# A transformer block with windowed attention and routed experts: the first block's program order, and scatters tied to steps

## The chip, the cores and the metric

The kernel runs on one core of a Trainium2 chip. Its engines work beside each other, each through its own queue in order: TensorE (PE) for matrix products, VectorE (DVE) and ScalarE (ACT) for elementwise work and reductions, GpSimd (POOL), and SyncE (SP), which here only issues transfers. The metric is device time in microseconds (us); the time before is 508.23, the median of six runs from 506.51 to 510.97.

## The reference

The input is x, 2048 rows of 256 values. A vector c gives six modulation vectors of 256. Cut to what matters:

```
mod = (silu(c) @ wmod).reshape(1, 6, 1, -1)
sa, ca, ga, sb, cb, gb = ...            # ga, gb are kept away from zero
h = layernorm(x) * (1 + ca) + sa
x = x + ga * attention(h)               # 16 heads of 16, windows of 64 rows
h = layernorm(x) * (1 + cb) + sb
x = x + gb * (experts(h) + shared(h))   # 16 experts, each row goes to 4
```

In the attention each chunk of 64 rows looks at itself and the chunk before. The experts are gated two-layer networks with 176 hidden values; the router chooses four of 16 for each row, with a weight. The shared network has 352 hidden values and takes every row.

## The kernel before

The rows are worked in four blocks of 512 (`NB`), each as four tiles of 128 rows (`NT`). The kernel is written as one stream of instructions; a framework then decides in which order each engine gets them, by dependences, by a model of when inputs are ready and by the place in the program. So an instruction that is ready early can stand on its engine ahead of others that come before it in the program. Waits between engines are added by the framework.

**Constants and loads** (L114 to L290): masks, identity matrices, counters, then the loads on SP's queue, then `sc`, the silu of c.

**`norm_t`** (L227) is a generator. It takes statistics of a block's four tiles (`bn_stats`, `bn_aggr`, L233 and L234, DVE), yields, takes the square root on ACT (L236) and the reciprocal on DVE, writes `xn` (L241), yields, and per half of 128 columns transposes on PE (L249) and writes `hT` on ACT with the modulation's shift and scale (L250). `half` is 0 for the norm ahead of the attention and 1 for the one ahead of the experts.

**`shift_scale`** (L299) computes shift and scale of one half: 16 matmuls (L304), two DVE instructions that write `mod` (L310, L311).

**`front(b)`** (L352) runs `norm_t` and then the projections of block b: queries (L363, evicted by DVE L368 and ACT L369), keys (L374, L378) and values (L393, evicted by ACT L397 and DVE L398, L399). They share two PSUM buffers of the tag "mm".

**The attention loop** (L683) has 16 units per block, 64 in all. `scores(u)` handles two units: a mask matmul each (L450) and the products (L456). `softmax(u)` takes row maxima into `top` (L472, four buffers), subtracts them or hands them to ACT, and takes the exponential (L477, L485). `total`, `turn_p`, `spread`, `turn_s`, `values` and `heads_out` finish the heads. Beside the units the loop advances two generators by one step or two: `nexts`, which is `front` of the next block, and `ends`, which is first `gates` (the second half of the modulation and the gate vectors) and then `back` of the block before.

**`back(b)`** (L556) applies the output projection, norms again, routes the rows and computes for each row and choice a place `at` (L658) in the table `slots` in memory. A row of `slots` holds 256 normed values, 16 weights and four words for the token number: `RW` is 276, and only the first of the four is read later. Sixteen indirect transfers per block (four tiles, four choices, L664) scatter the rows `row` into `slots` from POOL's queue, with a yield ahead of every second one. The helper `apart` tells the framework that these do not depend on each other.

**After the loop** (L712 to L765) the expert weights `wgu` are loaded, and `shared(b)` (L403), the shared network of blocks 0 to 2, is advanced as the generator `side`, two steps for each step of `ends`; its matmuls are L413 and L424. Then the rows per expert are counted and a table of expert blocks is made.

**The expert stage** (L768 to L891): SP fills the ends of the expert lists with blank rows (L788), loads blocks of 128 rows from `slots` (`xr`, L803), each load behind all writes of `slots`. The shared network of block 3 runs, then 79 expert blocks: transpose (L814), up (L832), transpose (L846), down (L854), and an indirect transfer from POOL that adds the result into one of two sums (L861). At the end the sums are read back and added to x (L900 to L912).

Of the kernel before, what the change touches and what calls it, by code (L numbers as in the profile page):

```python
# [8 lines left out]
F32 = mybir.dt.float32  # L9
# [8 lines left out]
P = 128  # L18
# [5 lines left out]
NT = TB // P  # L24
# [6 lines left out]
def adaln_block_kernel(  # L31
# [17 lines left out]
    nc = tc.nc  # L49
    S = x.shape[0]  # L50
    NB = S // TB
    NE = extra_scale.shape[1]
    TOPK = 4
# [7 lines left out]
    RS = S + P  # L61
    NBLK = S * TOPK // P + NE - 1
    RW = E + NE + 4
# [9 lines left out]
    xs = []  # L73
# [37 lines left out]
        return w.rearrange("(k p) n -> p k n", p=P)  # L111


    ident = const.tile([P, P], F32, name="ident")  # L114
    make_identity(nc, ident)
    eps_b = const.tile([P, 1], F32, name="eps_b")
# [5 lines left out]
    for par in range(2):  # L122
# [9 lines left out]
        out=mask[0:W], in_=mask[0:W], compare_op=ALU.is_ge, fill=NEG, base=0,  # L132
# [3 lines left out]
        out=mask[0:W], in_=mask[0:W], compare_op=ALU.is_ge, fill=NEG, base=W,  # L136
# [10 lines left out]
    for h in range(2):  # L147
# [7 lines left out]
        out=before, in_=before, compare_op=ALU.is_gt, fill=0.0, base=0,  # L155
# [38 lines left out]
    slots = dram.tile([RS * NE + P, RW], F32, name="slots")  # L194
# [4 lines left out]
    def apart(ins, name):  # L199

        ins = getattr(ins, "ins", ins)
        tc.declare_no_dep(ins, group=name, reason="no two of these write one row")
        tc.add_to_no_dep_group(name, ins)
        written[name].append(ins)
# [22 lines left out]
    def norm_t(pool, psum, xb, half, dst, xn=None):  # L227

        mv = pool.tile([P, NT, 2], F32, tag="mv", name="mv")
        rstd = pool.tile([P, NT], F32, tag="rstd", name="rstd")  # L230
        for t in range(NT):
            st = pool.tile([P, 6], F32, tag="st", name="st")
            nc.vector.bn_stats(st, xb[:, t, :])  # L233
            nc.vector.bn_aggr(mv[:, t, :], st)  # L234
        yield
        nc.scalar.activation(rstd, mv[:, :, 1], AF.Sqrt, bias=eps_b[:, 0:1])  # L236
        nc.vector.reciprocal(rstd, rstd)
        if xn is None:
            xn = pool.tile([P, NT, E], F32, tag="xn", name="xn", bufs=1)
        for t in range(NT):  # L240
            nc.vector.tensor_scalar(  # L241
                xn[:, t, :], xb[:, t, :], mv[:, t, 0:1], rstd[:, t : t + 1],
                ALU.subtract, ALU.mult,
            )
        for k in range(KC):
            yield
            ps = psum.tile([P, NT, P], F32, tag="mm", name="ps_xt")
            for t in range(NT):
                nc.tensor.transpose(ps[:, t, :], xn[:, t, k * P : (k + 1) * P], ident)  # L249
            nc.scalar.activation(  # L250
                dst[:, k, :], ps[:, :, :].rearrange("p t q -> p (t q)"), AF.Identity,
                bias=mod[:, 3 * half, k : k + 1], scale=mod[:, 3 * half + 1, k : k + 1],
            )
# [29 lines left out]
    for acc in sums_of:  # L283
        nc.sync.dma_start(
            out=acc[:, :].rearrange("(n p) e -> p n e", p=P),
            in_=blank[:, 0:E].unsqueeze(1).to_broadcast([P, S // P + 1, E]),
# [12 lines left out]
    def shift_scale(psum, half):  # L299
        ps = psum.tile([P, 2, KC], F32, tag="mm", name="ps_mod")  # L300
        for i in range(2):
            for m in range(KC):
                for k in range(KC):
                    nc.tensor.matmul(  # L304
                        ps[:, i, m : m + 1],
                        lhsT=wmod_at(3 * half + i, k)[:, m * P : (m + 1) * P],
                        rhs=sc[:, k : k + 1],
                        start=(k == 0), stop=(k == KC - 1),
                    )
        nc.vector.tensor_copy(mod[:, 3 * half, :], ps[:, 0, :])  # L310
        nc.vector.tensor_scalar(mod[:, 3 * half + 1, :], ps[:, 1, :], 1.0, None, ALU.add)  # L311
# [29 lines left out]
    with ExitStack() as actx:  # L341
        wa = actx.enter_context(tc.tile_pool(name="wa", bufs=2))
# [60 lines left out]
        def shared(b, hidden, psum):  # L403

            hs = []
            for j in range(SJ):
                n = min(P, SH - j * P)
                h = hidden()
                hs.append(h)
                pg, pu = psum(), psum()  # L410
                for ps, w in ((pg, sg), (pu, su)):
                    for k in range(KC):
                        nc.tensor.matmul(  # L413
                            ps[0:n], lhsT=w[:, k, j * P : j * P + n], rhs=hT[b][:, k, :],
                            start=(k == 0), stop=(k == KC - 1),
                        )
                    yield
                nc.scalar.activation(h[0:n], pg[0:n], AF.Silu)
                nc.vector.tensor_tensor(h[0:n], h[0:n], pu[0:n], ALU.mult)
            for t in range(NT):  # L420
                ps = psum()[:, 0:E]
                for j in range(SJ):
                    n = min(P, SH - j * P)
                    nc.tensor.matmul(  # L424
                        ps, lhsT=hs[j][0:n, t * P : (t + 1) * P], rhs=sd[0:n, j, :],
                        start=(j == 0), stop=(j == SJ - 1),
                    )
                nc.vector.tensor_tensor(xs[b][:, t, :], ps, xs[b][:, t, :], ALU.add)
                yield

        UNITS = 4 * 2 * KC
        probs, sums, turned, scale, av, outs = {}, {}, {}, {}, {}, {}

        def where(u):

# [24 lines left out]
        def softmax(u):  # L464

            g, r = divmod(u, 4)
            s = probs[u]
            if r == 0:
                sums[g] = wa.tile([P, 4, 4], F32, tag="sum", name="sum")
            alone = r % 2 == 1  # L470
            top = wa.tile([P, 4], F32, tag="top", name="top", bufs=4)
            nc.vector.tensor_reduce(top, s, AX.X, ALU.max, negate=alone)  # L472
            sm = wa.tile([P, 4, 2 * W], F32, tag="sm", name="sm", bufs=4)
            probs[u] = sm
            if alone:
                for n in range(4):
                    nc.scalar.activation(  # L477
                        sm[:, n, :], s[:, n, :], AF.Exp, bias=top[:, n : n + 1],
                        accum_out=sums[g][:, n, r : r + 1],
                    )  # L480
                return
            nc.vector.tensor_tensor(
                sm, s, top[:, :].unsqueeze(2).to_broadcast([P, 4, 2 * W]), ALU.subtract
            )
            nc.scalar.activation(sm, sm, AF.Exp)  # L485
# [70 lines left out]
        def back(b):  # L556

            oT = outs.pop(b)
            for t2 in range(NT // 2):
                ps = ps_mm.tile([P, 2, E], F32, tag="mm", name="ps_a")  # L560
                for t in range(2):
                    at = (2 * t2 + t) * P
# [94 lines left out]
            at = wr_.tile([P, NT, TOPK], I32, tag="at", name="at", bufs=2)  # L657
            nc.vector.tensor_scalar(at, keys[:, :, 0:TOPK], -1.0, BIG, ALU.mult, ALU.add)  # L658
            nc.vector.tensor_tensor(row[:, :, E : E + NE], sr, chosen, ALU.mult)
            for t in range(NT):  # L660
                for i in range(TOPK):
                    if i % 2 == 0:
                        yield
                    ins = nc.gpsimd.indirect_dma_start(  # L664
                        out=slots[:, :],
                        out_offset=bass.IndirectOffsetOnAxis(ap=at[:, t, i : i + 1], axis=0),
                        in_=row[:, t, :],
                        in_offset=None,
                        bounds_check=RS * NE - 1,
                    )  # L670
                    apart(ins, "slots")


        heads = {}
        shift_scale(ps_mm, 0)
        for _ in front(0):
            pass
        last = NB * UNITS
        scores(0)
        softmax(0)  # L680
# [2 lines left out]
        for u in range(last + 3):  # L683
            if u % UNITS == 0 and u // UNITS + 1 < NB:
                nexts = front(u // UNITS + 1)
            if u % 2 == 0 and u + 2 < last:
                if (u + 2) % UNITS == 0:
                    for _ in nexts:
                        pass
                scores(u + 2)  # L690
            if u + 2 < last:
                softmax(u + 2)
            if u < last:
                total(u)
                turn_p(u)
            g, r = divmod(u, 4)
            if r == 3 and u < last:
                spread(g)
            if r == 0 and g > 0:
                turn_s(g - 1)  # L700
            if r == 1 and g > 0:
                values(g - 1)
            if r == 2 and g > 0:
                heads_out(g - 1)
                if g % (UNITS // 4) == 0:
                    for _ in ends:
                        pass
                    ends = back(g // (UNITS // 4) - 1)
            next(nexts, None)
            for _ in range(2 if r == 3 else 1):  # L710
                next(ends, None)
        nc.sync.dma_start(out=wgu, in_=w_gu_t.rearrange("(k p) e n -> p k e n", p=P))  # L712


# [8 lines left out]
        side = beside()  # L723
        for _ in ends:
            next(side, None)
            next(side, None)


        ps = ps_mm.tile([P, NE], F32, tag="mm", name="ps_n")
# [224 lines left out]
```

## Time and profile before

| | |
|---|---|
| median of six runs | 508.23 us |
| the profiled execution | 507.85 us |
| its span | 506.1 us |
| mean granted PE clock | 0.972 |
| first softmax instruction | 29.42 us |
| first reduction of units 16, 32, 48 | 70.5, 120.7, 169.9 us |
| scatters on POOL | 114.4 to 266.2 us, in four runs of sixteen |
| first `xr` load issued | 278.23 us |
| expert blocks on PE | about 281 to 479 us, 2.49 us each |

The span runs from the program's first instruction to its last; what the device's time has beyond it lies around it. All places in the text are microseconds from the start of the span. In the lines of the profile an engine's name is followed by the kernel's line, the instruction, what it writes and reads, the number of instructions merged (x), and in brackets the idle time of that engine just before and what ended it. PEld is PE's loading of weights, which runs beside its products. In the table of stretches the columns are the stretch, its length, and the busy time of each engine with the number of its instructions, then the granted PE clock, the share of the transfer engines and GB/s.

### The profile page before, as it was taken

How to read it: one execution, taken by the hardware profiler on the slowest of the kernel's cores; microseconds unless marked ns; L12 is line 12 of the kernel's file. 1: busy time of each engine (PE TensorE's matmuls, PEld its weight loads, DVE VectorE, ACT ScalarE, POOL GpSimd, SP SyncE). 2: the span in 40 equal slices, each digit the busy share in tenths (PEclk: the TensorE clock that was granted, in tenths of full speed). 3: DMA queues.
4: the chain of work that ended last, by engine and by line, in shares of the span. 5: the costliest groups of instructions: out<-in, count | busy, mean ns of one | idle time of the engine just before them, and what ended most of it. 6: DMA issues, size and time to landing. Idle time of an engine off the chain costs nothing.

```text
span 506.1 us, 9444 instructions
## 1 busy us (share of the span) xinstructions
PE 455.9 (90%) x2903; PEld 323.1 (64%) x2921; DVE 337.4 (67%) x913; ACT 226.2 (45%) x623; POOL 191.7 (38%) x166
## 2 busy tenths in 40 slices
PE   3999979998998899899999999999999999999900
PEld 3475766666766577556554677777777777777600
DVE  4599789789969898755333566666666666666515
ACT  2377687958866878742001233333333333333100
POOL 2002000007501730362470165756556566656720
PEclk9999999999999899999999999999999999999955
DMA  8968000002200310194135497677777767765487
GB/s 277 328 151 286 17 1 2 1 1 93 90 1 12 113 58 2 52 418 166 57 111 191 97 154 124 113 112 115 108 104 114 107 106 111 114 97 62 55 239 289
DMA packets 52563, 58.87 MB, mean 116 GB/s; under 512 B 16363, under 2 KB 48331, under 8 KB 52171
## 3 DMA queue, kind: packets, MB, share of 16 engines
q1 hardware_dynamic: 36435, 35.72, 25.5%
q0 software_dynamic: 14448, 19.41, 22.1%
q10 hardware_dynamic: 1632, 3.15, 1.7%
q8 instruction: 24, 0.39, 0.3%
q14 instruction: 24, 0.20, 0.1%
HBM read 29.90 MB, written 28.35 MB: 115 GB/s over the span
## 4 chain that ended last, share of the span: by engine, by line
PE 60%; DMA 18%; DVE 13%; ACT 5%; issue 3%; DVEq 0%; SPq 0%; POOLq 0%; ACTq 0%; POOL 0%
DMA sum<-y,xr 15%; PE pgu L832 12%; PE py L854 8%; PE pz L413 8%; PE pz L424 4%; PE pt L497 3%; PE s L456 3%; DVE top L472 3%; PE ps_q L363 3%; ACT sm L477 2%; PE px L814 2%; PE ph L846 2%; PE ps_a L564 2%; DMA got<-sum 2%; PE ps_k L374 2%
## 5 line engine op out<-in xcount | busy, mean ns | idle before, releaser
L861 POOL DMA_INDIRECT sum<-y,xr x79 | 122.2, 1547 | 96.4 <-DVE xT L820 41.5
L664 POOL DMA_INDIRECT slots<-row,at x64 | 63.0, 985 | 156.5 <-DVE at L658 109.0
L832 PE MATMUL pgu<-wgu,xT 128*128 x316 | 106.5, 460 | 0.4 <-DVE xT L820 0.4
L854 PE MATMUL py<-wd,hT 88*128 x316 | 81.4, 379 | 0.1
L816 ACT ACTIVATE xT<-px,mod 128x128 f32<-128x128 f32 x79 | 36.1, 457 | 81.4 <-PE px L814 79.3
L832 PEld LDWEIGHTS pgu<-wgu,xT 128*128 128x128 f32 x316 | 53.8, 190 | 17.4 <-ACT xT L816 0.7
L848 DVE COPY hT<-ph 88x256 f32<-88x256 f32 x79 | 33.2, 421 | 39.8 <-PE ph L846 39.8
L854 PEld LDWEIGHTS py<-wd,hT 88*128 88x128 f32 x316 | 53.6, 190 | 4.8 <-DVE hT L848 0.5
L838 ACT ACTIVATE h<-pgu 128x176 f32<-128x176 f32 x79 | 25.1, 317 | 59.3 <-PE pgu L832 59.3
L477 ACT ACTIVATE sm<-s,top 128x128 f32<-128x128 f32 x128 | 45.8, 371 | 10.8 <-DVE top L472 10.8
L497 PE MATMUL pt<-ident,sm 128*128 128x128 f32 x256 | 40.9, 282 | 7.4 <-ACT sm L485 6.1
L820 DVE TENSOR_SCALAR xT<-px,mod 128x128 f32<-128x128 f32 x79 | 32.4, 410 | 22.2 <-ACT xT L816 22.2
L499 ACT COPY pT<-pt 128x512 f32<-128x512 f32 x64 | 37.5, 593 | 19.0 <-PE pt L497 18.6
L472 DVE TENSOR_REDUCE top<-s 128x4 f32<-128x512 f32 x64 | 42.1, 681 | 2.9 <-PE s L456 2.6
L456 PEld LDWEIGHTS s<-wgu 32*128 32x128 f32 x512 | 31.8, 186 | 16.0 <-issue 15.6
L860 DVE TENSOR_TENSOR y<-py,gate 128x256 f32<-128x256 f32 x79 | 33.6, 425 | 11.7 <-PE py L854 1.0
L456 PE MATMUL s<-wgu 32*128 32x128 f32 x512 | 39.0, 285 | 0.1
L497 PEld LDWEIGHTS pt<-ident,sm 128*128 128x128 f32 x256 | 28.9, 141 | 15.7 <-ACT sm L485 7.3
L846 PEld LDWEIGHTS ph<-ident,h 128*88 128x88 f32 x158 | 19.4, 123 | 21.9 <-issue 13.5
L839 DVE SCALAR_TENSOR_TENSOR h<-h,by,pgu 128x176 f32<-128x176 f32 x79 | 30.3, 384 | 1.3 <-ACT h L838 1.3
L814 PE MATMUL px<-ident,xr 128*128 128x128 f32 x158 | 30.4, 273 | 0.3 <-DMA xr<-slots 0.3
L846 PE MATMUL ph<-ident,h 128*88 128x128 f32 x158 | 30.2, 273 | 0.0
(166 smaller groups left out, 670.2 us busy)
## 6 DMA issues: line engine op xcount, KB each, us to landing
xr<-slots SPq DMA_DIRECT2D x79, 138.0 KB
wgu<-in_w_gu_t SPq DMA_DIRECT2D x1, 5632.0 KB
sum<-blank SPq DMA_DIRECT2D x2, 2176.0 KB
wd<-in_w_down_t SPq DMA_DIRECT2D x1, 2816.0 KB
slots<-blank SPq DMA_DIRECT2D x17, 138.0 KB
x<-in_x SPq DMA_DIRECT2D x4, 512.0 KB
got<-sum SPq DMA_DIRECT2D x4, 512.0 KB
got<-sum ACTq DMA_DIRECT2D x4, 512.0 KB
```

What stands on the lines that cost most here:

```text
L413: nc.tensor.matmul(ps[0:n], lhsT=w[:, k, j * P : j * P + n], rhs=hT[b][:, k, :], start=(k == 0), stop=(k == KC - 1),)
L456: nc.tensor.matmul(probs[u + i][:, n, :], lhsT=qz[at, m, ch].rearrange("p h q -> p (h q)"), rhs=kT[at, m, ch * W : (ch + 2) * W], start=False,
L472: nc.vector.tensor_reduce(top, s, AX.X, ALU.max, negate=alone)
L477: nc.scalar.activation(sm[:, n, :], s[:, n, :], AF.Exp, bias=top[:, n : n + 1], accum_out=sums[g][:, n, r : r + 1],)
L497: nc.tensor.transpose(pt[:, n, :], p[:, n, :], ident)
L499: nc.scalar.copy(turned[u], pt)
L664: ins = nc.gpsimd.indirect_dma_start(out=slots[:, :], out_offset=bass.IndirectOffsetOnAxis(ap=at[:, t, i : i + 1], axis=0), in_=row[:, t, ...
L814: nc.tensor.transpose(ps[:, k, :], xr[b][:, k * P : (k + 1) * P], ident)
L832: nc.tensor.matmul(ps, lhsT=xT[b][:, k, :], rhs=wgu[:, k, bass.ds(e, 1), :].rearrange("p e n -> p (e n)"), start=(k == 0), stop=(k == KC - 1),
L846: nc.tensor.transpose(ps[:, c2, :], h[b][:, c2 * DH : (c2 + 1) * DH], ident)
L854: nc.tensor.matmul(ps, lhsT=hT2[b][:, c2, :], rhs=wd[:, c2, bass.ds(e, 1), :].rearrange("p e n -> p (e n)"), start=(c2 == 0), stop=(c2 == 1),)
L861: nc.gpsimd.indirect_dma_start(out=sums_of[b % NA][:, :], out_offset=bass.IndirectOffsetOnAxis(ap=xr[b][:, E + NE : E + NE + 1].bitcast(I3 ...
```

## The change

Cut to its core:

```diff
+    first_order = ctx.enter_context(ExitStack())
+    first_order.enter_context(tc.manual_schedule(
+        engines={mybir.EngineType.PE, mybir.EngineType.DVE, mybir.EngineType.Activation}
+    ))
     ident = const.tile([P, P], F32, name="ident")
...
-            nc.vector.bn_stats(st, xb[:, t, :])
+            ins = nc.vector.bn_stats(st, xb[:, t, :])
+            if half == 0 and xb is not xs[0]:
+                tc.keep_in_program_order(ins)
...
-                    yield
+                    yield hs[-2][:, 0:1] if j else None
...
-                yield
+                yield xs[b][:, t, 0:1]
...
-            top = wa.tile([P, 4], F32, tag="top", name="top", bufs=4)
+            top = tops[u] = wa.tile([P, 4], F32, tag="top", name="top", bufs=6)
...
-            for t in range(NT):
-                for i in range(TOPK):
-                    if i % 2 == 0:
-                        yield
-                    ins = nc.gpsimd.indirect_dma_start(
...
+            sends.extend((at, row, t, i) for i in range(TOPK) for t in range(NT))
+        sends = []
+        def send(after=None):
+            at, row, t, i = sends.pop(0)
+            if after is not None:
+                nc.gpsimd.tensor_copy(row[0 : after.shape[0], t, RW - 1 : RW], after)
+            ins = nc.gpsimd.indirect_dma_start(
...
         heads = {}
+        starts = front(0)
+        next(starts)
+        next(starts)
         shift_scale(ps_mm, 0)
-        for _ in front(0):
+        for _ in starts:
             pass
+        first_order.close()
...
             for _ in range(2 if r == 3 else 1):
                 next(ends, None)
+            for _ in range(min(len(sends), 2 if r == 3 else 1)):
+                send(tops[min(u + 2, last - 1)][:, 0:1])
...
         for _ in ends:
             next(side, None)
-            next(side, None)
+            done = next(side, None)
+            for _ in range(min(len(sends), 2)):
+                send(done)
+        while sends:
+            done = next(side, None)
+            send(done)
```

`manual_schedule` makes PE, DVE and ACT take the instructions from the first constant to the last value of block 0 in the program's order. Within that stretch the statistics and `xn` of block 0 now come ahead of `shift_scale`. `keep_in_program_order` puts an instruction behind the one that the program has just before it on the same engine; here these are the statistics of blocks 1 to 3 ahead of the attention.

The scatters are no longer steps of `back`. They go into a list, choice by choice with the four tiles in turn, and are taken from it beside the loop: one per unit, two in each fourth unit, and after the loop with the steps of `side`. Ahead of a scatter POOL copies one value per row from a tile that this step has just made (`top`, a hidden tile or x) into the last, unread word of the row that is scattered. So the scatter can't be issued before that step. `top` has six buffers in place of four.

More of the change, by code (lines that the diff above doesn't have):

```diff
@@ L428, in shared @@
                 nc.vector.tensor_tensor(xs[b][:, t, :], ps, xs[b][:, t, :], ALU.add)
-                yield
+                yield xs[b][:, t, 0:1]
         UNITS = 4 * 2 * KC
-        probs, sums, turned, scale, av, outs = {}, {}, {}, {}, {}, {}
+        probs, tops, sums, turned, scale, av, outs = {}, {}, {}, {}, {}, {}, {}
         def where(u):
@@ L659, in back @@
             nc.vector.tensor_tensor(row[:, :, E : E + NE], sr, chosen, ALU.mult)
-            for t in range(NT):
-                for i in range(TOPK):
-                    if i % 2 == 0:
-                        yield
-                    ins = nc.gpsimd.indirect_dma_start(
[L665 to L671, printed above, removed]
+            sends.extend((at, row, t, i) for i in range(TOPK) for t in range(NT))
[5 more added lines that the diff above has]
+            ins = nc.gpsimd.indirect_dma_start(
+                out=slots[:, :],
+                out_offset=bass.IndirectOffsetOnAxis(ap=at[:, t, i : i + 1], axis=0),
+                in_=row[:, t, :],
+                in_offset=None,
+                bounds_check=RS * NE - 1,
+            )
+            apart(ins, "slots")
         heads = {}
+        starts = front(0)
+        next(starts)
+        next(starts)
         shift_scale(ps_mm, 0)
-        for _ in front(0):
+        for _ in starts:
             pass
+        first_order.close()
         last = NB * UNITS
```

## The prediction, made blind

> **What bounds the kernel now.** I read the page first, then the chain of waits in order of time, then the timeline of the first 36 us, then the busy time by block of rows. The profiled execution took 507.85 us: its span of 506.1 and 1.75 around it. The runs shown have a median of 508.23, so 0.38 is added to a sum made on this execution.
>
> ```profile
> PE 455.9 (90%) x2903; PEld 323.1 (64%) x2921; DVE 337.4 (67%) x913; ACT 226.2 (45%) x623; POOL 191.7 (38%) x166
> PE 60%; DMA 18%; DVE 13%; ACT 5%; issue 3%; DVEq 0%; SPq 0%; POOLq 0%; ACTq 0%; POOL 0%
> ```
>
> TensorE (PE) is busy for 90% of the span, so only its idle 50 us can be won. By stage: from 205 to 479 us PE runs nearly without gaps (shared experts, then 2.49 us per expert block), and the last 19 us are transfers. The change touches neither, so what it gains by 205 us should arrive at the end nearly one to one. What is left is the start and the attention. The chain of waits shows the start (start, length, what):
>
> ```profile
> 6.53 3.56 PE ps_mod L304 x16
> 11.07 0.73 DVE xn L241 x2
> 14.58 1.28 PE s L450 x3
> 15.86 3.99 PE ps_q L363 x8
> ...
> 22.29 0.73 DVE st L233 x2
> 23.24 1.28 DVE xn L241 x4
> 26.02 1.99 PE ps_v L393 x8
> 28.02 1.12 PE s L456 x24
> ```
>
> Two things delay block 0. After the modulation matmuls the norm's `xn` is still to come. And at 22 to 24.5 us the chain runs through statistics and `xn` of later blocks on VectorE (DVE), ahead of block 0's value copies. The timeline shows why the norm is late:
>
> ```profile
> 10.11 0.16 DVE L310 COPY mod<-ps_mod 128x2 f32<-128x2 f32 x1 [3.19 <-PE ps_mod L304]
> 10.19 0.15 DVE L311 TENSOR_SCALAR mod<-ps_mod 128x2 f32<-128x2 f32 x1
> 10.26 0.24 DVE L234 BATCH_NORM_AGGREGATE mv<-st 128x2 f32<-128x6 f32 x2
> ...
> 10.53 0.30 ACT L236 ACTIVATE rstd<-mv,eps_b 128x4 f32<-128x4 f32 x1 [6.40 <-DVE mv L234]
> ...
> 29.42 1.29 DVE L472 TENSOR_REDUCE top<-s 128x4 f32<-128x512 f32 x2
> ```
>
> The last two aggregates stand behind the copy of `mod`, for which DVE waits 3.19 us; they needed nothing from it. The first softmax instruction starts at 29.42.
>
> **The start, step by step.** In program order all DVE constants come first. The last of GpSimd's (POOL) iotas they need ends at 3.77; with `blank`, `taken` and the four small `sc` steps DVE reaches the statistics at about 5.2 (before 5.06, released by x landing). Four pairs of 0.414 + 0.167 end at 7.6; square root 0.30, reciprocal 0.17 and four `xn` of 0.396 end near 9.8. PE's modulation matmuls still run from 6.53 to 10.08, now beside this. Four transposes (0.60 in a warm group of four) end at 10.75, and ScalarE (ACT) writes the two halves of `hT` by 12.3 (2 x 0.78). The first query matmul needs one half only: 11.7 in place of 15.65. Query and key matmuls keep their 7.6 us from there (23.22 less 15.65), so values start at 19.3. A value tile is evicted by 0.37 on ACT and 0.42 + 0.43 on DVE, one behind the other, so four take 4.9: 24.2 at the latest, 23.4 where a buffer is free, before 28.0. The first scores follow with two masks (0.407 each) and 16 matmul records (1.16): the first softmax at 25.3. **Gain there: 4.1 us.**
>
> Not all of it is kept. Before, PE had put four mask matmuls (2.1 us) into gaps at 13.5 to 15.9 and had also done the second pair of scores by 29.1. From 10.1 to 61 us it was busy 48.0 of 50.9 us. The same work is due in both programs, so PE can save at most 2.9 there, unless its busy time includes hidden waiting. I take 2.9 and keep 0 and 4.1 as ends.
>
> **The norm of later blocks.** Before, the statistics of blocks 1 and 2 ran at 20.5 to 27.4, and `xn` of block 1 at 23.2; block 3 ran one block ahead too. `keep_in_program_order` puts each into its own block of the attention. Per block that is 4 x (0.414 + 0.167) + 0.17 + 4 x 0.396 = 4.1 us of DVE work. Block 0's stage gains block 1's norm and loses block 2's `xn` (1.6), block 1's stage swaps one norm for another, block 2's stage gains block 3's. ACT changes its tables for the square root and back:
>
> ```profile
> 83.70 1.28 ACT L236 ACT_TABLE_LOAD   x1
> ...
> 87.26 1.28 ACT L477 ACT_TABLE_LOAD   x1 [1.00 <-DVE top L472]
> ```
>
> The square roots of blocks 1 and 2 were free of this, at 22.41 and 27.43, ahead of the first exponential. Now one more pair falls into block 0 and one more into the later stages: 4 x 1.28 = 5.1 us of ACT. The price of one late norm with its pair of loads can be read from blocks that differ by just that (columns: length, then busy time of PE, PEld, DVE, ACT, POOL):
>
> ```profile
> 29.40:70.50 41.10, 39.10 (x361) 28.20 (x366) 35.56 (x69) 31.13 (x102) 2.55 (x3) 1.00 0.43 127
> 70.50:120.70 50.20, 45.60 (x426) 33.44 (x433) 44.28 (x126) 38.49 (x113) 5.06 (x5) 1.00 0.04 13
> 120.70:169.90 49.20, 46.02 (x435) 33.57 (x443) 42.78 (x119) 37.58 (x112) 17.20 (x20) 1.00 0.14 50
> ```
>
> The windows run from one block's first softmax to the next one's. Block 1 held a norm ahead and its extra loads, block 2 did not: 50.2 against 49.2. So a late norm costs 1.0, since PE's projections lie beside it. Bounds: 0, where PE covers it; 4.1 + 2.56 = 6.7, where DVE and ACT work lies end to end. I take 0.6 for block 0 (it loses `xn` of block 2) and 1.0 for block 2.
>
> The Trainium skill ("ScalarE: Activation LUTs", What ACT_TABLE_LOAD costs and Table sets: the hidden batching unit) speaks against this edit: exponentials and roots should be batched, and a switch is put at 2.66 us with its drain. By that page, as an estimate, the four loads would be 10.6 us of ACT. In this trace the square root follows the 1.28 us load by 0.02 (83.70 to 85.00), with no drain to be seen.
>
> **The scatters.** Nothing in the view of waits waits long for one. DVE's reduction took 0.684 us beside a scatter (19 of them) and 0.679 without (38); spreading them frees nothing. Added: up to 62 POOL copies of 128x1. The nearest rows are POOL's 128x1 memset, 0.10, and its 128x16 copy, 0.19. A scatter took 0.98 + 0.30 before the next, so the pace goes from 1.28 to about 1.6. The copy writes the row that the scatter four places earlier reads, so it waits for that landing; behind it on POOL stand only further scatters. Landing has a median of 2.7, less than four paces; under the weight load at 213 to 233 it is up to 13.7, and POOL waited there before too. Block 3's sixteen would end near 245.9 + 16 x 1.6 = 271.5 and land by 274.5; the first `xr` load was issued at 278.23, behind the blanks of SP. So cost 0, with 3.7 us of cover; without it each late us would be one at the end. The six `top` buffers give DVE six units before a reused buffer waits for POOL's copy: 0. The `wgu` load and SP's other DMAs keep their places.
>
> **Sum:** -2.9 + 0.6 + 1.0 + 0 = -1.3. 507.85 - 1.3 + 0.38 = **506.9** as a median.
>
> **Rivals.**
> 1. *The start is kept whole.* For it: attention is not held by one engine (PE 92%, DVE 87% of 61 to 205), and the chain lost time in 22 to 24.5 that now goes. The norms cost 0 and 4.1 stays: 504.1. Against it: PE's 2.9 us of idle time.
> 2. *The late norms become the bound (slower).* Where no projections lie beside the softmax, DVE is the chain: from 115 to 135 it is busy 18.93 of 20 us. If half the 6.7 is paid twice, 6.7 - 2.9 = +3.8: 512.0. It decides from a price of 1.5 per late norm on (2 x 1.5 = 2.9). Against it: the 1.0 between blocks 1 and 2.
> 3. *The scatters end late.* If POOL needs 2.1 us per scatter, block 3's land at 245.9 + 33.6 + 2.7 = 282.2, 4.0 after the load's old place: 510.9 with the rest of the sum.
> 4. *It does not do what it says:* the modulation still leads or the freed order puts other work in between; 0 at the start, +1.0 later: 509.2.
>
> **How the numbers follow.** Forecast 0.45, rival 1 0.28, rival 2 0.18, rival 3 0.04, rival 4 0.05. The forecast's own range is 504.5 to 509.5. Eight in ten need rival 1 and most of rival 2: 503.0 to 512.0. 0.5% is 2.5 us, about what a measurement of this kernel can tell from no change. Faster than 505.7: nearly all of rival 1 and 0.1 of the forecast, 0.36. Slower than 510.8: rivals 2 and 3 and 0.03 of the forecast, 0.24. Between: 0.40.
>
> **What would show it.** Right: the square root of block 0 near 7.9 instead of 10.53; first query matmul near 11.7; first softmax near 25.3; no statistics of blocks 1 to 3 before it; two more pairs of table loads; unit 16's reduction (70.5 before) at 67 to 69.6; from then on a shift that shrinks by about 1 in block 2. Wrong: unit 16 at or after 70.5 (rival 2), PE waiting for `xr` after its last shared matmul (rival 3), statistics still standing early (rival 4). The prediction fails as a whole if the freed engines are ordered anew in the attention so that blocks 1 to 3 change by more than 2 us.

## The result and the profile after

The changed kernel takes 519.32 us, median of 20 runs (511.80 to 522.02), beside 509.13 of the kernel before: a ratio of 1.0135, 95% interval 1.0106 to 1.0164. By this ratio it is slower by about 6.9 us, by the medians by 10.2; 506.9 was forecast, and the median lies above the range. The ratio leaves out the executions that ran longest, which had the lowest granted clock, and the profiled execution is one of these (519.78 us, span 518.0).

The page of the changed kernel: the row of busy time, and the chain that ended last.

```profile
PE 471.9 (91%) x2907; PEld 332.8 (64%) x2921; DVE 337.1 (65%) x913; ACT 232.2 (45%) x627; POOL 203.6 (39%) x224
PE 41%; DMA 38%; DVE 10%; ACT 4%; issue 3%; SPq 2%; DVEq 0%; POOL 0%; POOLq 0%; ACTq 0%
```

PE is busy 16.0 us longer with nearly the same instructions, so it is not more work; the mean granted clock is 0.952 in place of 0.972. How much of the 16.0 is the clock, and how much is waiting inside the busy time, the page does not tell. ACT has 6.0 more (5.1 of it four table loads), POOL 11.9 (58 copies).

The start did what the change says (rows of the timeline; `...` stands for rows left out):

```profile
8.03 0.30 ACT L243 ACTIVATE rstd<-mv,eps_b 128x4 f32<-128x4 f32 x1 [3.92 <-DVE mv L241]
...
10.05 0.16 DVE L317 COPY mod<-ps_mod 128x2 f32<-128x2 f32 x1
...
12.19 4.65 PE L370 MATMUL ps_q<-hT,wqkv 128*128 128x512 f32 x8
...
26.11 1.29 DVE L479 TENSOR_REDUCE top<-s 128x4 f32<-128x512 f32 x2
```

The first softmax comes 3.3 us earlier. The loss comes after it. Stretches from one block's first softmax to the next one's (the stretch, its length, then the busy time of PE, PEld, DVE, ACT and POOL with their instructions, the granted clock, the share of the transfer engines and GB/s):

```profile
26.11:76.58 50.47, 47.23 (x365) 32.48 (x368) 38.73 (x78) 34.33 (x105) 2.63 (x3) 0.86 0.39 112
76.58:129.46 52.88, 48.78 (x431) 35.73 (x438) 44.51 (x130) 39.52 (x113) 6.90 (x12) 0.97 0.04 15
129.46:181.30 51.84, 47.97 (x428) 35.30 (x433) 43.44 (x127) 38.58 (x113) 18.37 (x33) 0.97 0.12 42
```

Block 0 takes 9.4 us longer than before, blocks 1 and 2 take 2.7 and 2.6. In block 0 the clock is granted at 0.86. The expert blocks still take PE 199.0 us from first to last (198.5 before), as the prediction said. The timeline of block 0 shows the late norm of block 1:

```profile
30.50 0.42 DVE L238 BATCH_NORM_STATS2 st<-x 128x6 f32<-128x256 f32 x1
...
36.41 1.28 ACT L243 ACT_TABLE_LOAD   x1
...
37.71 0.30 ACT L243 ACTIVATE rstd<-mv,eps_b 128x4 f32<-128x4 f32 x1
38.03 1.28 ACT L484 ACT_TABLE_LOAD   x1
...
38.92 2.61 DVE L248 TENSOR_SCALAR xn<-x,mv,rstd 128x256 f32<-128x256 f32 x4
39.79 0.44 PE L256 MATMUL ps_xt<-ident,xn 128*128 128x128 f32 x2 [1.50 <-DVE xn L248]
...
46.81 6.11 PE L370 MATMUL ps_q<-hT,wqkv 128*128 128x512 f32 x8
```

The same query matmuls in the kernel before:

```profile
40.66 1.98 PE L363 MATMUL ps_q<-hT,wqkv 128*128 128x512 f32 x4 [0.33 <-ACT hT L250]
...
44.02 1.98 PE L363 MATMUL ps_q<-hT,wqkv 128*128 128x512 f32 x4
```

The statistics of block 1 begin at 30.5, one by one between softmax steps. The square root follows at 37.71, PE waits for `xn`, and the block's first query matmul comes 20.7 us after the first softmax, where it took 11.2 before. It then runs mostly at half clock, 6.11 us for eight records in place of 4.0.

### The profile page after: what moved, and what is told of

Same layout as the page of the kernel before. It is cut to its first block, busy times and chain, and to the rows that moved or that the text cites. A ratio compares the mean times of both kernels' runs of the same rounds, so it can differ in the third digit from the quotient of the medians.

```text
span 518.0 us, 9564 instructions
## 1 busy us (share of the span) xinstructions
PE 471.9 (91%) x2907; PEld 332.8 (64%) x2921; DVE 337.1 (65%) x913; ACT 232.2 (45%) x627; POOL 203.6 (39%) x224
## 3 DMA queue, kind: packets, MB, share of 16 engines
q10 hardware_dynamic: 1632, 3.15, 1.6%
## 4 chain that ended last, share of the span: by engine, by line
PE 41%; DMA 38%; DVE 10%; ACT 4%; issue 3%; SPq 2%; DVEq 0%; POOL 0%; POOLq 0%; ACTq 0%
DMA sum<-y,xr 34%; PE pz L420 6%; PE s L463 4%; PE pt L504 4%; PE ps_q L370 3%; PE pz L431 3%; PE ps_k L381 3%; DVE top L479 3%; PE pgu L860 2%; PE ps_a L571 2%; PE av L540 2%; PE ps_xt L256 2%; PE ps_v L400 2%; ACT sm L484 2%; DMA got<-sum 2%
## 5 line engine op out<-in xcount | busy, mean ns | idle before, releaser
L679 POOL COPY row<-top 128x1 f32<-128x1 f32 x44 | 8.5, 206 | 123.5 <-DVE top L479 117.1
L463 PEld LDWEIGHTS s<-wgu 32*128 32x128 f32 x512 | 35.7, 189 | 18.6 <-issue 18.4
L504 PE MATMUL pt<-ident,sm 128*128 128x128 f32 x256 | 42.0, 292 | 6.0 <-ACT sm L492 5.5
L463 PE MATMUL s<-wgu 32*128 32x128 f32 x512 | 44.5, 291 | 0.1
L504 PEld LDWEIGHTS pt<-ident,sm 128*128 128x128 f32 x256 | 30.9, 149 | 13.5 <-ACT sm L492 6.6
```

The costliest lines, as they stand in the source:

```text
L463: nc.tensor.matmul(probs[u + i][:, n, :], lhsT=qz[at, m, ch].rearrange("p h q -> p (h q)"), rhs=kT[at, m, ch * W : (ch + 2) * W], start=False,
L504: nc.tensor.transpose(pt[:, n, :], p[:, n, :], ident)
```

## The experiments

All ratios are to the kernel before, run beside it on the same chip, with 95% intervals; the chip differs from one group of kernels to the next. A trace is of one execution. Line numbers shift with the edits.

### First: one part of the change at a time

`order_only`: the ordered start alone; statistics not pinned, scatters as before. `keep_only`: the kernel before with the pin alone:

```
+            ins = nc.vector.bn_stats(st, xb[:, t, :])
+            if half == 0 and xb is not xs[0]:
+                tc.keep_in_program_order(ins)
```

`ties_only`: the kernel before with the list of scatters, the tying copies and six `top` buffers. `order_keep`: the changed kernel with the scatters as before.

> The changed kernel with two of its three parts undone: only the program order up to block 0's values, with the norm ahead of the modulation, is kept. Theory A (the late norms of blocks 1 to 3 make lulls on TensorE, and after a lull the granted clock falls to 0.5): the norms may stand early here, so the first softmax starts near 26 us, two or no extra pairs of table loads appear, the clock stays at 1.00 up to 160 us, and the time is 2 to 4 us under the kernel before. Theory B (the dense start itself brings the halved clock): the clock falls to 0.5 between 25 and 55 us here too and the time is 3 to 10 us over. Theory C (the tied scatters cost the time): like A.

> The kernel before with the pin on the statistics of blocks 1 to 3 alone. Theory A: no statistics of blocks 1 to 3 ahead of block 0's softmax, 20 table loads in place of 16, unit 16's reduction later by 3 or more, halved clock somewhere in 30 to 60 us in part of the executions, 3 to 10 us over the kernel before. Theories B and C: within 2 us of the kernel before, since a late norm costs about 1.

> The kernel before with the scatters taken from a list, tied to steps by the padding column, and six top buffers. Theories A and B: within 2 us of the kernel before. Theory C: 5 us or more over.

> The changed kernel with its scatters as before (steps of back, four top buffers). Theories A and B: the time of the changed kernel within 3 us, 511 to 520, with the clock at 0.5 in stretches of block 0. Theory C: 505 to 508.

| kernel | median, us | ratio | blocks 0, 1, 2 in the trace, us |
|---|---|---|---|
| order_only | 512.17 | 1.0105 (1.0065 to 1.0144) | 43.0, 51.6, 49.1 |
| keep_only | 519.21 | 1.0203 (1.0148 to 1.0258) | 44.6, 54.1, 51.3 |
| ties_only | 509.31 | 1.0048 (1.0020 to 1.0075) | 42.6, 51.6, 49.2 |
| order_keep | 515.17 | 1.0120 (1.0071 to 1.0169) | 50.6, 53.0, 53.0 |

The pin alone costs at least as much as the whole change (12.5 us by the medians, more than theory A's 3 to 10); by the middle values it costs more, and the ordered start gives something back, but the intervals overlap. Alone, the ordered start loses for a reason of its own: its first softmax starts at 33.19, 3.8 us after that of the kernel before. Its timeline:

```profile
15.72 0.43 DVE L238 BATCH_NORM_STATS2 st<-x 128x6 f32<-128x256 f32 x1 [7.74 <-DMA x<-in_x]
...
17.00 2.21 PE L254 MATMUL ps_xt<-ident,xn 128*128 128x128 f32 x8 [5.91 <-DVE xn L246]
```

Without the pin the statistics of block 1 stand on DVE ahead of block 0's `xn`; DVE waits 7.74 us for block 1's x, and PE for DVE. So, as the kernel stands, the ordered start needs the pin. By the letter `order_only` came out as theory B had it (clock at 0.5 from 34.9 to 38.4 us, 5.5 us over by the medians), and theory A's forecast of a gain failed. The half-clock piece speaks for B less than it seems, since the kernel before has one too in a second profile (below), and the late start accounts for 3.8 of the 5.5; what rules B out is `first_early`, further down.

For the scatters, a second profile of the kernel before (`before_2`, below) has the same two pieces at half clock as `ties_only`, one in block 0 and one in block 1. `before_2`, then `ties_only`:

```profile
29.77:72.39 42.62, 41.10 (x365) 29.49 (x366) 35.71 (x70) 31.07 (x102) 2.55 (x3) 0.96 0.41 122
72.39:123.95 51.56, 47.83 (x432) 34.70 (x433) 44.26 (x127) 38.67 (x112) 5.09 (x5) 0.97 0.04 13
```

```profile
29.71:72.33 42.62, 40.62 (x361) 29.55 (x366) 35.70 (x69) 31.12 (x102) 2.54 (x3) 0.96 0.40 121
72.33:123.93 51.60, 47.24 (x427) 34.82 (x434) 44.27 (x127) 38.75 (x112) 5.67 (x10) 0.97 0.04 13
```

At the same clock the ties cost nothing that a trace shows (spans 508.4 and 508.0; first `xr` load at 280.4 and 280.7). The timed runs say 0.5%, 2.6 us between the medians, a little over the 2 us that theories A and B allowed; apart from some lost clock (15.0 us against 13.7 in the median) it has no place in the record.

### Second: the norm off the chain, step by step

`first_half` moves block 1's statistics into the ordered start, behind the keys, and pins the square root to its old place; `first_early` moves the square root too:

```
+        for i, _ in enumerate(starts):
+            if i == 5:
+                mv1 = take_stats(wa, xs[1], True, "1")
+                stats[1] = mv1, root(wa, mv1, "1")
```

`norm_ahead` also takes the norms of blocks 2 and 3 in the middle of the block two ahead; `ahead_no_ties` is that with the scatters as before:

```
+            b2 = u // UNITS + 2
+            if b2 < NB and u % UNITS == 8:
+                mv2 = take_stats(wa, xs[b2], True)
+            if b2 < NB and u % UNITS == 9:
+                ready[b2] = normed(wa, xs[b2], mv2, root(wa, mv2))
```

> The changed kernel, but the statistics of block 1 stand in the ordered start, behind the keys, where VectorE sat idle (about 17.9 to 21 us); the square root of block 1 and its two table loads stay where they are, one step into block 0. Theory A1 (the late norm costs VectorE time in a stretch where VectorE is busy without a gap): block 0, 50.5 us from the first softmax to unit 16 after the change against 41.1 before, falls to 45 to 47, and the time to 1.004 to 1.009 of before (after: 1.0135). Theory A2 (it is the two table loads that hold the exponentials): block 0 falls by less than 1.5 us and the time stays at 1.010 or above. Theory B (the ordered start itself makes the clock halve behind it): the half-clock pieces between 27 and 52 us stay, 10 us in all, and the time at 1.010 or above.

> The changed kernel with statistics and square root of block 1 in the ordered start, while the square root's table is still loaded: two table loads fewer (18 where the changed kernel has 20). Blocks 2 and 3 keep their late, pinned norms. Theory A (a norm that stands directly ahead of its block's projections is on the chain): first softmax at 26 to 28 us, block 0 at 41 to 44 us where it took 50.5, the half-clock piece at 41.5 to 51.7 gone; time 0.999 to 1.006 of before. Against the run with only the statistics moved it tells the price of the two loads: A1 says less than 1 us between them, A2 more than 2. Theory B: 1.010 or above.

> As the run before, and the whole norm of blocks 2 and 3 (statistics, square root with its two table loads, normalized x) stands pinned in the middle of the block two ahead (steps 8 and 9 of 16), where VectorE has gaps: the same instructions and table loads as there, but not ahead of their own block's projections. Theory A: blocks 1 and 2 lose the 2 to 4 us that each late norm cost; time 0.993 to 1.000 of before. Theory C (loads and statistics cost what they take wherever they stand inside the blocks): the same as the run before within 0.3%.

> As the run before, with the scatters as in the kernel before the change. Theory A with the measured price of the tied scatters (1.0048 alone): 0.4 to 0.5% faster than the run before, 0.989 to 0.996 of before. If the tied scatters only cost beside a late norm or not at all: the same as the run before within 0.2%.

### Third: the table loads alone, fewer loads, no ties

`loads_only` is `first_early` with a square root that nobody reads:

```
+            if u == 1:
+                spare = wa.tile([P, NT], F32, tag="spare", name="spare")
+                tc.keep_in_program_order(nc.scalar.activation(
+                    spare, mv1[:, :, 1], AF.Sqrt, bias=eps_b[:, 0:1]))
```

`one_pair` is `ahead_no_ties` with one square root for blocks 2 and 3 in block 0. `untied` is `norm_ahead` with `send()` without its argument.

> The run with block 1's statistics and square root in the ordered start (1.0038), with one thing added: one step into block 0, where the changed kernel takes block 1's square root, a square root that nobody reads, pinned there. It brings both table loads back (20 in all) without anything waiting for its result. Between that run and the one that left the square root there (1.0113) lies 0.75%, 3.8 us. If the loads alone cost it, by holding ScalarE for 2.9 us: 1.009 to 1.012. If the cost is that the normalized x, and so the block's projections, wait for the square root: 1.003 to 1.006. Between them: both.

> The fastest run so far (norms ahead, scatters as before, 0.9906) with one square root of 128x8 for blocks 2 and 3 in the middle of block 0 instead of two of 128x4: 16 table loads instead of 18, block 3's statistics moved 48 us up with it. If a table load off the chain still costs its 1.28 us: 2.6 us less, 0.985 to 0.988. If what is off the chain costs next to nothing: 0.989 to 0.992. The 2.3 us of statistics that come into block 0 could cost up to that: 0.992 to 0.995.

> The run with all norms ahead and tied scatters (0.9946), with the copies into the padding column left out: the scatters keep their new list, but nothing ties them to a step. If the ties (copies on GpSimd that wait for a maximum, and maxima kept longer) cost the 0.4 to 0.5% of the tied scatters: 0.990 to 0.992. If it is the order of the list (first all four tiles' first choice) or the extra buffers of the maxima: 0.994 to 0.996.

| kernel | median, us | ratio | blocks 0, 1, 2 in the trace, us |
|---|---|---|---|
| first_half | 512.91 | 1.0113 (1.0075 to 1.0151) | 45.4, 51.5, 52.8 |
| loads_only | 511.71 | 1.0085 (1.0060 to 1.0111) | 43.0, 51.5, 51.3 |
| first_early | 509.20 | 1.0038 (1.0008 to 1.0069) | 41.1, 53.0, 51.3 |
| norm_ahead | 504.50 | 0.9946 (0.9916 to 0.9976) | 40.9, 48.4, 50.5 |
| ahead_no_ties | 503.69 | 0.9906 (0.9874 to 0.9939) | 42.4, 50.0, 50.4 |
| untied | 503.00 | 0.9934 (0.9900 to 0.9968) | 40.9, 49.9, 51.1 |
| one_pair | 506.52 | 0.9997 (0.9972 to 1.0021) | 42.1, 49.7, 49.1 |

Theory A holds: with the same statistics and the same start, the time falls below that of the kernel before once the norms stand off the chain. From `first_early` to `norm_ahead` neither an instruction nor a table load goes away, only the place changes, and 0.92% goes (4.7 us); theory C had them equal within 0.3%. Block 1 in `first_early`, with block 2's norm late in it, and in `norm_ahead`, with block 3's in its middle:

```profile
67.39:120.41 53.02, 48.74 (x431) 35.30 (x438) 44.54 (x130) 39.56 (x113) 6.87 (x12) 0.97 0.04 15
```

```profile
67.60:116.03 48.43, 44.88 (x420) 32.62 (x426) 42.91 (x124) 37.33 (x106) 5.15 (x8) 1.00 0.03 10
```

Of the 4.6 us between them one half-clock piece is some 1.4 (see the last section). Theory B falls too: `first_early` has the same dense start, its time is 1.0038 where B had 1.010 or above, and it lost no clock in block 0.

For block 1's norm, the table loads are the larger part by the middle values. `loads_only` brings back 0.47% of the 0.75% between `first_early` and `first_half`, a little under the band for loads alone; its interval overlaps with both, so the split is not sharp. Its timeline on ACT shows who is held:

```profile
33.28 1.28 ACT L756 ACT_TABLE_LOAD   x1
34.58 0.30 ACT L756 ACTIVATE spare<-mv,eps_b 128x4 f32<-128x4 f32 x1
34.89 1.28 ACT L515 ACT_TABLE_LOAD   x1
36.19 0.63 ACT L515 ACTIVATE sm<-sm 128x512 f32<-128x512 f32 x1
36.73 0.57 ACT L529 COPY pT<-pt 128x512 f32<-128x512 f32 x1
37.19 0.78 ACT L280 ACTIVATE hT<-ps_xt,mod 128x512 f32<-128x512 f32 x1
```

An exponential, the copy of the turned probabilities and the eviction of `hT` stand behind 2.9 us of loads and root (`hT` starts at 37.19, in `first_early` at 33.61); block 0 takes 43.0 in place of 41.1, with no half-clock piece in either.

Moving the statistics (`first_half`) met a part of each forecast: the time stayed at 1.0113, as A2 had it, and block 0 fell by 5.1 us to 45.4, as A1 had it. The clock tells the two apart. Call (1 - mean granted clock) x span the lost clock of an execution. In executions that lost at most 16.5 us of it, both kernels take 512.7 in the median (7 of 22 executions of the changed kernel, 5 of 6 of `first_half`; the kernel before took 509.13 and 507.84 beside them), so the statistics on DVE themselves explain little. But the other 15 executions of the changed kernel take 520.0, and the median lost clock falls from 22.0 to 15.1 us in `first_half`. The 5.1 us in block 0 are the size of the 10.2 us at half clock that its trace no longer has there. So the pinned statistics cost mostly by the clock, and the root with its loads cost with the clock kept as well.

Two expectations of this group missed. `one_pair` saves a pair of loads and was slower than `ahead_no_ties`, by more than the 2.3 us of statistics it brings into block 0; why is open. `untied` lies between its two bands, and its interval covers both: whether the ties or their order cost 0.4% is not settled.

### Fourth: is it the lull that halves the clock?

Over 22 executions of the changed kernel a straight line through span and lost clock is 499.4 us + 0.80 x the lost clock, correlation 0.95; the lost clock runs from 14.3 to 26.0 us. In the median the kernel before loses about 14, the changed one 22. Some 11 to 13 us of that lie at the span's end, where PE has nothing left to do (clock 0.50 from 495.5 us on in the changed kernel's trace). `warm` fills PE's lull, the stretch of block 0 where PE waits for `xn`, and the same place in blocks 1 and 2:

```
+            if half == 0 and xb is not xs[0] and k == 0:
+                for _ in range(4):
+                    nc.tensor.matmul(
+                        ps, lhsT=ident, rhs=mv[:, :, 1].unsqueeze(2).to_broadcast([P, NT, P]),
+                        start=True, stop=True)
```

> The changed kernel with four matmuls more in each of blocks 1 to 3, between the statistics and the transposes of x, where TensorE has its lull (38.3 to 39.8 us in block 0): 128x512 out of the identity and a broadcast of the variances, into the bank that the transposes then overwrite, so nothing of the result changes. They add about 1.8 us of TensorE time to each block. If the half-clock pieces follow from TensorE's lulls: lost clock ((1 - mean granted clock) times span) falls from a median of 22 us to 17 or less, and the time to 1.010 or less in spite of the added work. If they come from the dense start or from something else: lost clock stays at 20 or more, and the time at 1.013 to 1.025.

> The changed kernel once more, unaltered, on the same chip as the run with the four added matmuls: 1.011 to 1.016, lost clock 18 to 24 us.

Here every kernel ran longer: the kernel before took 558.62 us, `warm` 534.09 (ratio 0.955, 0.9505 to 0.9594) and the changed kernel 533.60 (0.9539, 0.9495 to 0.9583). The ratios of these runs say nothing about the change. The kernel before lost 42 us of clock there in the median, 28 more than else (granted clock 0.922 to 0.929), the changed one 29, 7 more; there is no trace of the kernel before from these runs, and the reason is not known. The next three are from another chip:

> The kernel with the four added matmuls per block once more, since in the last call every kernel, the one before too, ran 3 to 10% longer than ever before. If the half-clock pieces follow from TensorE's lulls: lost clock at a median of 17 us or less and 1.010 or less; if not: 20 us or more and 1.013 to 1.025.

> The changed kernel unaltered beside it: 1.011 to 1.016 of before, lost clock 18 to 24 us, where the chip is as it was in the first three calls; 0.95 to 0.96 if it is as in the last.

> The kernel before, for a profile of this call's chip: 505 to 509 us as in the first three calls, or 556 to 563 as in the last; in that case its trace shows which of its waits grew by 50 us.

There the times were as at first: `before_2` 508.84 (0.9989, 0.9956 to 1.0021), `after_3` 519.10 (1.0148, 1.0083 to 1.0213), `warm_2` 521.37 (1.0241, 1.0193 to 1.0289). Median lost clock: 14.2, 21.7 and 20.0 us. The stretches of the changed kernel and, below, of `warm_2` around the lull:

```profile
36.00:41.50 5.50, 3.62 (x58) 2.55 (x54) 5.50 (x13) 5.25 (x13) 2.63 (x3) 0.99 0.58 150
41.50:52.00 10.50, 10.50 (x27) 5.45 (x26) 5.64 (x12) 5.02 (x14) 0.00 (x0) 0.52 0.90 316
```

```profile
36.00:41.50 5.50, 5.48 (x22) 2.57 (x21) 5.50 (x15) 5.22 (x10) 1.56 (x2) 1.00 0.59 161
41.50:52.00 10.50, 10.50 (x90) 6.65 (x90) 8.49 (x16) 6.93 (x22) 1.06 (x2) 1.00 0.89 313
```

With the lull filled, the half-clock piece behind it is gone (in the trace of `warm` too) and block 0 takes 47.2 us in place of 50.5. The transfer engines are as busy in both (0.90 and 0.89), so they do not make the difference. But the added matmuls took about 3.7 us of PE in block 0, twice the estimate, they changed PE's order, and blocks 1 and 2 grew to 54.2 and 54.3. For the whole kernel, 1.0241 and 20.0 us of lost clock lie in the band of the other reading, that the lulls are not the cause. And a lull alone is not enough. The trace of `keep_only` has one with even less work for PE (busy 0.40 of its emptiest 3.41 us; 0.45 in the changed kernel), and the clock behind it stays at 1.00:

```profile
39.00:42.00 3.00, 1.15 (x28) 0.64 (x16) 3.00 (x8) 2.96 (x10) 2.12 (x3) 1.00 0.45 145
42.00:52.00 10.00, 9.81 (x46) 5.41 (x47) 9.21 (x17) 7.10 (x20) 0.52 (x1) 1.00 0.95 333
```

So for block 0 the lull is a cause in some executions and not in others, and what decides between them is not shown; for the lost clock of the later blocks the lull is not shown as the cause.

## Why the prediction was wrong

The sum was -2.9 + 0.6 + 1.0 + 0 = -1.3; measured is +6.9 by the ratio and +10.2 by the medians.

**The start, -2.9: right in size, not in its reason.** Square root 8.03 (7.9 forecast), first query matmul 12.19 (11.7), first softmax 26.11 (25.3). So 3.3 us came of the 4.1 forecast at the first softmax; 0.5 of the missing 0.8 lie ahead of the first query matmul. In `first_early`, where block 0 holds no late norm, unit 16 starts its reduction at 67.39, 3.2 us before the old place: the 3.15 us won at its first softmax are still there, and the cap of 2.9 by PE's idle time did not bind. That 2.9 is near 3.2 is partly luck, a cap that did not hold and a gain smaller than forecast. Rival 1 was right that the start is kept whole.

**The late norms, +0.6 and +1.0: this step failed.** The step was "So a late norm costs 1.0, since PE's projections lie beside it", read from 50.2 against 49.2. The extra norm in that block 1 was block 3's, a block ahead of its projections. The row priced a norm's work where nobody waits for its result, and the pin takes away just that distance. Late, the norm stands ahead of its own block's projections, and exponentials and the eviction of `hT` queue behind its table loads. It also breaks the "swap" of block 1, taken as nothing.

Measured: block 1's norm in block 0 costs 0.97% (`first_early` to the changed kernel), 4.9 us, clock included; `first_early`'s blocks 1 and 2 take 2.8 and 2.2 longer than before, 5.0 together, one half-clock piece of some 1.4 among it. These are 9.9 for three norms, where 1.6 was forecast. With the clock kept it is less, by this estimate: the seven executions of the changed kernel that lost at most 16.5 us of clock take 512.7, 3.5 over the kernel before, and with the 3.2 of the start put back the three norms cost 6.7, or 2.2 each. Either way 1.5, from which rival 2 decides, is passed. The bound of 6.7 per norm holds for these shares, but block 0 of the profiled execution, with 13.65 us at half clock, grew by 9.4.

Rival 2 had the sign (+3.8 forecast), and its sign came: unit 16 starts at 76.58, after the old 70.5. So did the last one that the prediction names, blocks that change by more than 2 us (2.7 and 2.6). Rival 2's reason was DVE as the chain; the runs point to the root and its loads on ACT and to the clock more than to the statistics on DVE.

**The clock: no term at all.** Between `before_2` and `after_3` lie 7.5 us of lost clock; at 0.80 that is 6.0 of 10.3 us between their medians. It belongs to the late norm in good part: `first_half`, which only moves block 1's statistics, loses 15.1 us in the median.

**The scatters, 0:** at the same clock the trace agrees; the timed runs put at most 0.75% on them. The first `xr` load is issued at 291.8, and PE goes on to the expert blocks at 294.39 without a gap behind its last shared matmuls (its first transposes there wait 0.9 us for `xr` in all, 0.3 before), so rival 3 did not happen. A copy on POOL took 0.2 us, near the 0.19 of the row that the prediction went by.

Together: -3.2 + 4.9 + 5.0 = 6.7, and 0 to 2.4 for the ties, beside 6.9. This sum is less of a test than it looks: the 4.9 is itself a difference of measured times, so what it tests is `first_early` alone, -3.2 + 5.0 = 1.8 beside 1.9 measured (0.38%). The shares come from different groups of runs, each with an interval of some 0.3% either way. Two sums inside the prediction are rounded wrongly (2 x 1.5 is 3.0, and the parts of "slower" make 0.25); nothing rests on them.

## What to carry over

A price read from another block holds only if the same instructions wait for it: before using it, look where its result is needed and what queues behind it. An early part of a block that looks like clutter on the chain (statistics at 22 us) may be the slack of the next block; it can be moved into an idle stretch in the start, or half a block ahead, rather than pinned to where it is used. Here that gave 0.9906 (0.9874 to 0.9939) with the ordered start kept and the scatters as before, faster than both kernels. And where executions of one kernel differ by their clock, compare those that kept it with each other before explaining a difference of the whole.

## What the hardware showed that was not expected

The clock falls to 0.5 in pieces of 3.41 us or multiples, and one piece of 3.41 costs about 1.4 us (`before_2` has one in block 0 and one in block 1 where the first profile has none: 42.6 and 51.6 us in place of 41.1 and 50.2). Behind the lull of the changed kernel the piece was 10.2 us. PE was never idle for more than 1.5 us at a stretch there; it was busy 3.62 of 5.5. In the 18 traces of this study a window of 3.41 us with PE busy for about half (0.45 to 0.55) stands right ahead of 17 of the 31 pieces that begin between 40 and 180 us. But two of the 31 follow a window in which PE was busy throughout, and such a window also passed without a piece (the kernel before, 71.4 to 74.8 us, PE busy 1.65 of 3.41, clock 1.00 behind it). In 11 of the 18 traces a piece begins within 0.7 us of the end of the second half's modulation matmuls, which are one column wide (27.8 us in the changed kernel), though PE counts as busy all through them. So what makes a piece is not settled here.

The Trainium skill ("TensorE: Matmul & The Clock Gate", What's actually happening) describes a free-running window of 3413 ns after whose idling the clock halves; the length agrees with the 3.41 us pieces here. Its rule to avoid idle gaps of over about 3 us (Why this matters for your kernels) would have passed this lull; the trace shows halving behind gaps of at most 1.5 us, so the measurement decides.
